# Layer 0's start reordered: input in four transfers, constants moved behind the normalisation, SyncE's transfers in source order

## The chip, the core and the metric

The kernel runs on one core of a Trainium2 chip. The metric is the device time of one execution in microseconds, taken as the median over runs. Five engines work side by side, each on its own list of instructions: TensorE (PE, with its weight loads PEld), VectorE (DVE), ScalarE (ACT), GpSimd (POOL) and SyncE (SP). SP computes nothing here; it issues transfers, and so does ACT in a few places.

## The reference

Two transformer layers work on 2048 tokens of 256 numbers, all in float32. Each layer is an attention block and a feed-forward block, both with a layer normalisation in front and a residual addition behind.

```python
x = x + attn0(layernorm(x), w_project, w_out)            # causal, 16 heads of 16
x = x + ffn0(layernorm(x), router_w, router_b, expert_w, expert_b)   # 8 experts, top 2 per output
x = x + attn1(layernorm(x), w_qkv, w_proj)               # 16 query heads, 4 key/value heads of 128
x = x + ffn1(layernorm(x), gate, up, down)               # 4-bit weights, gelu(gate) * up
return x

def layernorm(x, eps=1e-5):
    return (x - mean(x)) / sqrt(var(x) + eps)

def attn0(x, w_project, w_out):
    q, k, v = split(x @ w_project.T)
    att = softmax(where(causal, q @ k.T / sqrt(16), -1e9))
    return (att @ v) @ w_out.T
```

Only the start of layer 0's attention is touched by the change.

## The kernel before, in words

The residual `xres` stays in SBUF for the whole run as 16 tiles of 128 tokens by 256. Four tiles make a block, and layer 0 has four blocks, numbered `j` = 0 to 3. For each block the kernel normalises (`norm_pieces`: statistics L180 and L181 on VectorE, the power -1/2 L185 on GpSimd, the scaling L194 to `xn` on VectorE), transposes on TensorE (`inputs_T`, L210), and projects to queries and keys (`project`, L545) and values (`values`, L567). `project` copies its product from PSUM into a tile `stage` (L549), and eight transfers (L555) then spread `stage` over the tile `qk`, 16 partitions each. For block 0 half of these transfers are issued by ScalarE, for the others all by SyncE.

The attention runs in 40 batches `n`. Each is `greatest` (scores, L647), `mask` (the causal mask on TensorE, L660, and the row maxima on VectorE, L666), `shift` (L676, L679), `powers` (scores again, L695, and the exponentials, L704) and `mixed` (L731); `divided` (L749 to L788) closes a head group. Between these, `fill` hands out pieces of other work (the next block's normalisation and projections, layer 0's feed-forward) by fixed budgets per slot, so the order of instructions on TensorE, VectorE, ScalarE and GpSimd is the order of the source: `manual_schedule(engines=order)` pins them. SyncE is not in that set. The scheduler may place its transfers anywhere that their data allow.

The work before the first batch, in source order: identity and small constants (`mask32` L86, `fold8` L91, `mask8` L95, of which the last two serve layer 1 only), VectorE's presets of `va` (L481) and `bs` (L497), GpSimd's presets of `qk`, three products on TensorE that nobody reads (`idle`, L795, on the weights `wp`), the normalisation of blocks 0 and 1 in a row, GpSimd's presets for block 1 and its splitting of the biases (L518 to L529), block 0's projections, then block 1's transposes, and the first batch's scores. Block 2's normalisation is handed out in the first `fill` of batch 1.

SyncE's loads are written at the end of the batches:

```python
if n < 4:
    w, dram = (rw, router_w) if n < 2 else (ew, expert_w)
    for i in range(4):
        load_pair(w, dram, 4 * n % 8 + i)
...
if n in (0, 2):
    load_x(n // 2 + 2)
```

`load_pair` pins each transfer behind the SyncE instruction that was traced just before it. So the four pairs of batches 0 and 2 stand behind the `qk` transfers of block 1, while `load_x(2)` and `load_x(3)`, which need nothing, and the pairs of batches 1 and 3, which are pinned only behind these, are placed early by the scheduler.

Of the kernel before, what the change touches and what calls it, by code (L numbers as in the profile page):

```python
# [32 lines left out]
def tile_transformer(  # L33
# [26 lines left out]
    def load_x(j):  # L60
        nc.sync.dma_start(
            out=xres[:, 4 * j : 4 * j + 4, :], in_=x[:, 4 * j : 4 * j + 4, :]
        )

    for t, eng in ((0, nc.sync), (2, nc.scalar)):
        eng.dma_start(out=xres[:, t : t + 2, :], in_=x[:, t : t + 2, :])
    in_order = ctx.enter_context(ExitStack())
    order = {
        mybir.EngineType.PE, mybir.EngineType.DVE, mybir.EngineType.Pool,
        mybir.EngineType.Activation,  # L70
    }
    in_order.enter_context(tc.manual_schedule(engines=order))
    ident = const.tile([P, P], F32, name="ident")
    make_identity(nc, ident)
    minus_half = const.tile([P, 4], F32, name="minus_half")
# [12 lines left out]
    )  # L88

    fold8 = const.tile([P, 8], F32, name="fold8")  # L90
    nc.vector.tensor_reduce(  # L91
        fold8, ident.rearrange("p (t b) -> p b t", b=8), AX.X, ALU.add
    )
    mask8 = const.tile([P, NS, 8], F32, name="mask8")
    nc.vector.tensor_copy(mask8, fold8.unsqueeze(1).to_broadcast([P, NS, 8]))  # L95

# [350 lines left out]
    with ExitStack() as l0:  # L449
# [28 lines left out]
                    mask32[:, i : i + 1].to_broadcast([P, 512]),  # L478
                )

        nc.vector.memset(va[:, :per_block], 1.0)  # L481
        nc.gpsimd.tensor_copy(
            qk[:, :, 0].rearrange("p g s q -> p g (s q)"),
            mask32[:, :4].unsqueeze(2).to_broadcast([P, 4, 512]),
# [9 lines left out]
            base=0, pattern=[[-1, P]], channel_multiplier=1,  # L494
        )
        bs = b1.tile([P, 2, 512], F32, tag="hi4", name="bs")
        nc.vector.memset(bs, 0.0)  # L497
        for i in range(3):
            nc.sync.dma_start(out=bs[32 * i : 32 * i + 8], in_=bias)
        rows = b1.tile([P, 12, P], BF16, tag="part", name="rows")  # L500
        sel = rows[:, :8]
        bp = rows[:, 8:].rearrange("p i q -> p (i q)")
# [1 line left out]
        def blanks(xn):  # L504

            after = b2.tile([P, 1], F32, tag="rs_v", name="after")
            nc.gpsimd.tensor_copy(after, xn[:, 3, 0:1])
            for i in range(2):
                nc.gpsimd.memset(maxes[i], 0.0)
            nc.gpsimd.memset(qk[:, :, NBLK + 1].rearrange("p g s q -> p g (s q)"), 0.0)  # L510
# [19 lines left out]

        def load_pair(w, dram, n):
            e, hc = divmod(n, 2)
            tc.keep_in_program_order(
                nc.sync.dma_start(
                    out=w[:, hc, 2 * e : 2 * e + 2],
                    in_=dram[hc * P : (hc + 1) * P, 2 * e : 2 * e + 2],
                )
            )

        def project(j, xT, half, stage, i):  # L540

            at = 256 * (1 - i) + 128 * half
            ps = ps_dn.tile([P, 512], F32, tag="dn", name=f"qk_ps{j}_{half}_{i}")
            for hc in range(2):
                nc.tensor.matmul(  # L545
                    ps, lhsT=wp[:, hc, at : at + P],
                    rhs=xT[:, hc].rearrange("p s q -> p (s q)"), start=hc == 0, stop=hc == 1,
                )
            nc.scalar.copy(stage[:, i], ps)  # L549
            if i:  # L550
                to = 4 + j % 2
                for r in range(8):
                    h = 32 * (r % 4)
                    eng = nc.scalar if j == 0 and r % 2 else nc.sync
                    eng.dma_start(  # L555
                        out=qk[h + 4 : h + 20, 2 * half + r // 4, j : to + 1 : to - j].rearrange(
                            "p i s q -> p i (s q)"
                        ),
                        in_=stage[16 * r : 16 * r + 16],
                    )  # L560

        def values(j, xT, s):

            ps = ps_dn.tile([P, 2, HID], F32, tag="dn", name=f"v_ps{j}_{s}")
            for i in range(2):
                for hc in range(2):
                    nc.tensor.matmul(  # L567
                        ps[:, i], lhsT=xT[:, hc, s + i], rhs=wp[:, hc, 512:768],
                        start=hc == 0, stop=hc == 1,
                    )  # L570
            at = j * per_block
            to = va[:, at : at + per_block].rearrange("p (s h d) -> p s h d", s=NS, d=17)
            nc.scalar.copy(
                to[:, s : s + 2, :, 0:16], ps.rearrange("p s (h d) -> p s h d", d=16)
            )

# [13 lines left out]
        def projections(j, xT):  # L590
            if j > 1:
                for s in (0, 2):
                    yield need("PE", 1.75, 1, cond=lambda: blanked > 5 * j - 10)
                    values(j, xT, s)
            for half in range(2):
                if j or half:
                    stage = a1.tile([P, 2, 512], F32, tag="stage", name=f"stage{j}_{half}")
                else:
                    stage = unused("stage0", "p (i q) -> p i q", i=2)
                for i in range(2):  # L600

                    yield need(
                        "PE", 1.75, 0 if half or i else 1,
                        cond=lambda: j < 2 or done >= 8 * j - 12 and blanked >= 5 * j - 5,
                    )
                    project(j, xT, half, stage, i)
                if half == (not j) and j < 2:
                    for s in (0, 2):
                        yield need("PE", 1.75)
                        values(j, xT, s)  # L610

        def prepare(j):

            out = []
            yield from norm_pieces(
                j, b1, b2, out, cond=lambda: j == 2 or inputs[2].next is None
            )
            xT = a1.tile([P, 2, NS, P], F32, tag="xT0", name=f"xT0_{j}")
            yield from inputs_T(j, out[0], xT)
            yield from projections(j, xT)  # L620

        def unused(name, pattern, **sizes):

# [167 lines left out]


        ps = ps_mm.tile([P, 4, P], F32, tag="mm", name="idle")
        for i in range(3):
            nc.tensor.matmul(  # L795
                ps.rearrange("p b q -> p (b q)"), lhsT=ident, rhs=wp[:, 0, :512],
                start=not i, stop=i == 2,
            )
        load_x(1)
        nc.sync.dma_start(out=wo, in_=w_out.rearrange("(k p) o -> p k o", p=P))  # L800
        both = [[], []]
        for j in range(2):
            for piece in norm_pieces(j, b1, b2, both[j]):
                pass
            normed.clear()
            if not j:
                blanks(both[0][0])
                xT = a1.tile([P, 2, NS, P], F32, tag="xT0", name="xT0_0")
                for piece in inputs_T(0, both[0][0], xT):
                    pass  # L810
        for i in range(5):
            blank(1, i)
        split_biases()
        for piece in projections(0, xT):
            pass
        xT = unused("xT0_1", "p (h s q) -> p h s q", h=2, s=NS)
        for piece in inputs_T(1, both[1][0], xT):
            pass
        greatest(0)
        mask(0)  # L820
# [7 lines left out]
        for n in range(NBT):  # L828
            j, s, gs = batches[n]
            if n in (1, 7):  # L830
                to = 2 if n == 1 else 3
                inputs[to] = Stream(prepare(to))
                streams.insert(0, inputs[to])
            if n + 1 < NBT and batches[n + 1][0] != j:
                while inputs[j + 1].next is not None:
                    fill(PE=2.0, DVE=2.0)
            with tc.high_priority(offset=AHEAD):
                if n + 1 < NBT:
                    greatest(n + 1)
                shift(n)  # L840
                if n + 1 < NBT:
                    mask(n + 1)

            fill(PE=(2.0, 2.0, 1.8, 1.6)[j], DVE=2.6)
            with tc.high_priority(offset=AHEAD):
                if n:
                    mixed(n - 1)
                powers(n)
            done += 1
            if n and batches[n - 1][2][-1] == 3:  # L850
                streams.insert(0, Stream(divided(*batches[n - 1][:2])))
            fill(PE=(2.4, 2.4, 2.2, 2.0)[j], DVE=2.6)
# [4 lines that stand above are left out]
                    loaded[n // 2, (4 * n % 8 + i) // 2] = slot  # L857
            for _ in range(1 + (n < 2) if blanked < 10 else 0):
                blank(2 + blanked // 5, (blanked + 4) % 5)
                blanked += 1  # L860
            if n in (0, 2):
                load_x(n // 2 + 2)
        mixed(NBT - 1)
        streams.insert(0, Stream(norm_pieces(0, b1, b2, normed_first)))
        last = Stream(divided(*batches[NBT - 1][:2]))
# [436 lines left out]
```

## Time and profile before

| what | value |
|---|---|
| median of 3 runs | 1177.23 us (1175.32 to 1181.05) |
| the profiled execution | 1182.05 us |
| its span, first to last instruction | 1180.3 us |
| mean granted TensorE clock | 0.993 |
| TensorE busy | 1148.1 us, 97% of the span |
| VectorE busy | 809.7 us, 69% |
| ScalarE busy | 484.3 us, 41% |
| GpSimd busy | 108.1 us, 9% |
| chain that ended last | PE 79%, DVE 15%, ACT 2%, issue 2%, POOL 1%, DMA 1% |

The profile is one execution, so its own time is what a sum of its durations is held against. A span that starts at 0 is the first instruction's start. Idle time of an engine counts only where the chain of waits passes through it.

### The profile page before, as it was taken

The page shows a single profiled execution, that of the slowest core. Times are in us where ns is not written, and L with a number is a line of the kernel's source. Part 1 is how long each engine was busy: PE and PEld are TensorE (multiplying, and loading weights), DVE is VectorE, ACT ScalarE, POOL GpSimd, SP SyncE. Part 2 cuts the span into 40 slices and gives each one's busy share as a digit, 9 for nine tenths or more (in the row PEclk, how much of TensorE's full clock was granted, in tenths as well). Part 3 has the DMA queues.
Part 4 walks back from the last instruction along what each step waited for, and adds up shares of the span by engine and source line. Part 5 has one row for each costly group of instructions (what it writes and reads, how often), then busy time and mean ns, then how long its engine had stood idle before and what let it go on. Part 6 is the DMA issues. An engine that isn't in the chain of part 4 may idle for free.

```text
span 1180.3 us, 18580 instructions
## 1 busy us (share of the span) xinstructions
PE 1148.1 (97%) x7178; PEld 663.9 (56%) x7178; DVE 809.7 (69%) x1783; ACT 484.3 (41%) x1099; POOL 108.1 (9%) x152
## 2 busy tenths in 40 slices
PE   7999989999999899999999999999999999999998
PEld 3656545555555445555555556565644465485487
DVE  5656869999989872867872685687599844725710
ACT  1434545555565453444444443555244312303300
POOL 7313212111111100000000000000000000000000
PEclk9989989999999999999999999999999999999999
DMA  7320010000000320000000001020020000000000
GB/s 217 68 67 12 10 28 1 1 1 2 2 1 2 113 66 1 1 1 1 1 1 1 1 1 45 19 58 24 21 50 3 0 1 18 0 1 18 1 13 23
DMA packets 21239, 26.46 MB, mean 22 GB/s; under 512 B 5128, under 2 KB 14600, under 8 KB 21152
## 3 DMA queue, kind: packets, MB, share of 16 engines
q1 hardware_dynamic: 20480, 24.10, 7.6%
q10 hardware_dynamic: 672, 1.18, 0.4%
q8 instruction: 56, 0.92, 0.3%
q14 instruction: 31, 0.25, 0.1%
HBM read 18.97 MB, written 2.10 MB: 18 GB/s over the span
## 4 chain that ended last, share of the span: by engine, by line
PE 79%; DVE 15%; ACT 2%; issue 2%; POOL 1%; DMA 1%; SPq 0%; ACTq 0%; DVEq 0%; POOLq 0%
PE qk_ps L982 11%; PE y L1229 9%; PE o L1073 9%; PE g L911 9%; PE u L911 9%; PE lg_ps L234 8%; PE eo L234 7%; DVE mx L666 3%; PE s L647 3%; PE s L695 3%; PE av L731 2%; PE qk_ps L545 2%; PE v_ps L964 2%; PE a L1053 1%; PE s L995 1%
## 5 line engine op out<-in xcount | busy, mean ns | idle before, releaser
L982 PE MATMUL qk_ps<-xT,wqkv 128*128 128x512 f32 x320 | 148.9, 599 | 2.3 <-ACT part L323 1.2
L234 PE MATMUL lg_ps<-rw,xT 128*128 128x512 f32 x256 | 122.5, 601 | 1.3 <-ACT xT L949 0.3
L234 PE MATMUL eo<-ew,xT 128*128 128x512 f32 x256 | 121.5, 600 | 0.8 <-ACT lg L297 0.5
L1073 PE MATMUL o<-wpj,oT 128*128 128x256 f32 x512 | 119.1, 382 | 0.0
L1229 PE MATMUL y<-wd,it 128*128 128x256 f32 x512 | 111.8, 379 | 0.0
L1073 PEld LDWEIGHTS o<-wpj,oT 128*128 128x128 f32 x512 | 95.9, 190 | 27.5 <-issue 14.3
L1229 PEld LDWEIGHTS y<-wd,it 128*128 128x128 f32 x512 | 97.0, 190 | 15.0 <-issue 2.2
L666 DVE TENSOR_REDUCE mx<-s 128x1 f32<-128x384 f32 (+3 forms) x176 | 100.4, 631 | 1.4 <-PE s L660 1.4
L982 PEld LDWEIGHTS qk_ps<-xT,wqkv 128*128 128x128 f32 x320 | 59.1, 190 | 71.4 <-issue 57.4
L704 ACT ACTIVATE pt<-s 128x512 f32<-128x512 f32 (+1 forms) x176 | 84.1, 564 | 36.3 <-PE s L695 36.3
L911 PE MATMUL g<-xT,wgu 128*128 128x512 f32 x192 | 90.4, 593 | 0.0
L911 PE MATMUL u<-xT,wgu 128*128 128x512 f32 x192 | 90.2, 592 | 0.0
L323 ACT ACTIVATE part<-eo,c 128x256 f32<-128x256 f32 x128 | 53.6, 472 | 84.7 <-PE eo L234 77.1
L714 POOL TENSOR_SCALAR_AFFINE_SELECT pt<-pt 128x256 f32<-128x256 f32 (+2 forms) x88 | 62.8, 720 | 261.9 <-ACT pt L704 261.3
L1207 ACT ACTIVATE th<-sq 128x512 f32<-128x512 f32 x64 | 40.3, 630 | 87.6 <-DVE sq L1206 87.6
L234 PEld LDWEIGHTS lg_ps<-rw,xT 128*128 128x128 f32 x256 | 46.1, 190 | 46.1 <-issue 37.3
L234 PEld LDWEIGHTS eo<-ew,xT 128*128 128x128 f32 x256 | 46.1, 190 | 45.7 <-issue 38.3
L222 DVE TENSOR_TENSOR xres<-xres,y 128x256 f32<-128x256 f32 x16 | 6.7, 421 | 92.5 <-PE y L1229 92.5
L185 POOL TENSOR_TENSOR ln_rs<-rs_v,minus_half 128x4 f32<-128x4 f32 x16 | 17.6, 1100 | 552.2 <-DVE rs_v L184 439.8
L297 ACT COPY lg<-lg_ps 128x512 f32<-128x512 f32 x64 | 37.6, 588 | 73.5 <-PE lg_ps L234 73.5
L1208 DVE SCALAR_TENSOR_TENSOR th<-th,g 128x512 f32<-128x512 f32 x63 | 43.1, 684 | 29.3 <-ACT th L1207 29.2
L911 PEld LDWEIGHTS u<-xT,wgu 128*128 128x128 f32 x192 | 36.5, 190 | 45.9 <-issue 44.7
(233 smaller groups left out, 1784.4 us busy)
## 6 DMA issues: line engine op xcount, KB each, us to landing
qk<-stage SPq DMA_DIRECT2D x56, 64.0 KB, 2.4
wqkv<-in_w_qkv SPq DMA_DIRECT2D x8, 320.0 KB, 6.6
rw<-in_router_w SPq DMA_DIRECT2D x8, 256.0 KB, 6.9
ew<-in_expert_w SPq DMA_DIRECT2D x8, 256.0 KB, 5.0
wpj<-in_w_proj SPq DMA_DIRECT2D x1, 2048.0 KB
out<-xres SPq DMA_DIRECT2D x4, 512.0 KB, 2.6
xres<-in_x SPq DMA_DIRECT2D x3, 512.0 KB, 8.5
dq_wgu<-in_gate_w SPq DMA_DIRECT2D x8, 128.0 KB, 2.4
```

The lines of the kernel that those rows point to most:

```text
L234: nc.tensor.matmul(ps, lhsT=xT[:, hc, (g % 4) * P : (g % 4 + 1) * P], rhs=w[:, hc, 2 * pair : 2 * pair + 2, :].rearrange("p e o -> p (e o) ...
L297: nc.scalar.copy(lg[:, 2 * pair : 2 * pair + 2, :].rearrange("p e o -> p (e o)"), ps)
L323: nc.scalar.mul(part[:, e % 4], ps[:, i], c[:, e : e + 1])
L666: nc.vector.tensor_reduce(maxes[n % 2][:, h, gs[0] : gs[0] + nb], ps[:, : nb * nk].rearrange("p (b k) -> p b k", b=nb), AX.X, ALU.max,)
L704: nc.scalar.activation(pt[:, i, : nb * nk], tiles[2 * pair + i][:, : nb * nk], AF.Exp, scale=0.25)
L714: nc.gpsimd.affine_select(out=last, in_=last, compare_op=ALU.is_ge, fill=0.0, base=0, pattern=pattern, channel_multiplier=-1,)
L911: nc.tensor.matmul(ps, lhsT=wgu[:, w, half, jj, par * P : (par + 1) * P], rhs=xT[:, half, :], start=half == 0, stop=half == 1,)
L982: nc.tensor.matmul(ps, lhsT=wqkv[:, hc, kv, h, :], rhs=xT[:, hc, :], start=hc == 0, stop=hc == 1,)
L1073: nc.tensor.matmul(ys[t // 2][:, t % 2], lhsT=state["o"][:, h, t * P : (t + 1) * P], rhs=wpj[:, HPK * kv + h, :], start=kv == 0 and h == 0 ...
L1207: nc.scalar.activation(th, sq, AF.Tanh, scale=0.7978845608028654)
L1208: nc.vector.scalar_tensor_tensor(th, th, 1.0, gp, ALU.add, ALU.mult)
L1229: nc.tensor.matmul(ps, lhsT=it[:, c // 2, c % 2, t * P : (t + 1) * P], rhs=wd[:, c // 2, c % 2, :], start=c == 0, stop=c == 2 * NJ - 1,)
```

## The change

Six edits. First, the four tiles of block 0 come in four transfers of one tile, two issued by SyncE and two by ScalarE, where there were two transfers of two tiles. Secondly, `fold8`, `mask8`, the preset of `bs` with its three transfers, and VectorE's preset of `va` move behind block 0's normalisation or further. Thirdly, block 0's normalisation is written out in two halves of two tiles, each with its own power on GpSimd. Fourthly, the products that nobody reads run on the identity instead of `wp`, five of them instead of three. Fifthly, block 1's normalisation is split around the first half of block 0's projections, and the copies of that block's second half and of its values go from ScalarE to VectorE. Sixthly, SyncE's transfers are pinned to the order of the source from the start to the end of batch 3, and `load_pair` no longer pins by itself.

```diff
-    for t, eng in ((0, nc.sync), (2, nc.scalar)):
-        eng.dma_start(out=xres[:, t : t + 2, :], in_=x[:, t : t + 2, :])
+    for t in range(4):
+        eng = nc.scalar if t % 2 else nc.sync
+        eng.dma_start(out=xres[:, t, :], in_=x[:, t, :])
...
+    loads_in_order = ctx.enter_context(ExitStack())
+    loads_in_order.enter_context(tc.manual_schedule(engines={mybir.EngineType.SP}))
...
     fold8 = const.tile([P, 8], F32, name="fold8")
-    nc.vector.tensor_reduce(
-        fold8, ident.rearrange("p (t b) -> p b t", b=8), AX.X, ALU.add
-    )
     mask8 = const.tile([P, NS, 8], F32, name="mask8")
-    nc.vector.tensor_copy(mask8, fold8.unsqueeze(1).to_broadcast([P, NS, 8]))
...
-        nc.vector.memset(va[:, :per_block], 1.0)
...
         bs = b1.tile([P, 2, 512], F32, tag="hi4", name="bs")
-        nc.vector.memset(bs, 0.0)
-        for i in range(3):
-            nc.sync.dma_start(out=bs[32 * i : 32 * i + 8], in_=bias)
...
-            tc.keep_in_program_order(
-                nc.sync.dma_start(
-                    out=w[:, hc, 2 * e : 2 * e + 2],
-                    in_=dram[hc * P : (hc + 1) * P, 2 * e : 2 * e + 2],
-                )
+            nc.sync.dma_start(
+                out=w[:, hc, 2 * e : 2 * e + 2],
+                in_=dram[hc * P : (hc + 1) * P, 2 * e : 2 * e + 2],
             )
...
-            nc.scalar.copy(stage[:, i], ps)
+            (nc.scalar.copy if j or not half else nc.vector.tensor_copy)(stage[:, i], ps)
...
-            nc.scalar.copy(
+            (nc.scalar.copy if j else nc.vector.tensor_copy)(
                 to[:, s : s + 2, :, 0:16], ps.rearrange("p s (h d) -> p s h d", d=16)
             )
...
+        def normed_by_twos():
+
+            xn = b1.tile([P, 4, HID], F32, tag="xn", name="xn0_0")
+            st = b2.tile([P, 4, 6], F32, tag="ln_st", name="ln_st0_0")
+            mv = b2.tile([P, 4, 2], F32, tag="ln_mv", name="ln_mv0_0")
+            roots = []
+            for two in (slice(0, 2), slice(2, 4)):
+                for t in range(two.start, two.stop):
+                    nc.vector.bn_stats(st[:, t, :], xres[:, t, :])
+                    nc.vector.bn_aggr(mv[:, t, :], st[:, t, :])
+                v = b2.tile([P, 4], F32, tag="rs_v", name=f"rs_v0_{two.start}")[:, :2]
+                rs = b2.tile([P, 4], F32, tag="ln_rs", name=f"ln_rs0_{two.start}")[:, :2]
+                nc.vector.tensor_scalar(v, mv[:, two, 1], EPS, None, ALU.add)
+                nc.gpsimd.tensor_tensor(rs, v, minus_half[:, :2], ALU.pow)
+                roots.append(rs)
+            for t in range(4):
+                nc.vector.tensor_scalar(
+                    xn[:, t, :], xres[:, t, :], mv[:, t, 0:1],
+                    roots[t // 2][:, t % 2 : t % 2 + 1], ALU.subtract, ALU.mult,
+                )
+            return xn
...
-        for i in range(3):
+        for i in range(5):
             nc.tensor.matmul(
-                ps.rearrange("p b q -> p (b q)"), lhsT=ident, rhs=wp[:, 0, :512],
-                start=not i, stop=i == 2,
+                ps, lhsT=ident, rhs=ident.unsqueeze(1).to_broadcast([P, 4, P]),
+                start=not i, stop=i == 4,
             )
         load_x(1)
         nc.sync.dma_start(out=wo, in_=w_out.rearrange("(k p) o -> p k o", p=P))
...
+        xn = normed_by_twos()
+        blanks(xn)
+        xT = a1.tile([P, 2, NS, P], F32, tag="xT0", name="xT0_0")
+        for piece in inputs_T(0, xn, xT):
+            pass
+        nc.vector.memset(bs, 0.0)
+        for i in range(3):
+            nc.sync.dma_start(out=bs[32 * i : 32 * i + 8], in_=bias)
+        nc.vector.memset(va[:, :per_block], 1.0)
+        second = []
+        norm_1 = norm_pieces(1, b1, b2, second)
+        for _ in range(3):
+            next(norm_1)
+        firsts_0 = projections(0, xT)
+        for _ in range(3):
+            next(firsts_0)
+        for piece in norm_1:
+            pass
+        normed.clear()
         for i in range(5):
             blank(1, i)
         split_biases()
-        for piece in projections(0, xT):
+        for piece in firsts_0:
             pass
+        nc.vector.tensor_reduce(
+            fold8, ident.rearrange("p (t b) -> p b t", b=8), AX.X, ALU.add
+        )
+        nc.vector.tensor_copy(mask8, fold8.unsqueeze(1).to_broadcast([P, NS, 8]))
         xT = unused("xT0_1", "p (h s q) -> p h s q", h=2, s=NS)
-        for piece in inputs_T(1, both[1][0], xT):
+        for piece in inputs_T(1, second[0], xT):
             pass
...
             if n in (0, 2):
                 load_x(n // 2 + 2)
+            if n == 3:
+                loads_in_order.close()
```

More of the change, by code (lines that the diff above doesn't have):

```diff
@@ L800, in tile_transformer @@
         nc.sync.dma_start(out=wo, in_=w_out.rearrange("(k p) o -> p k o", p=P))
[L801 to L810, printed above, removed]
+        xn = normed_by_twos()
[17 more added lines that the diff above has]
+        normed.clear()
         for i in range(5):
```

## The prediction

> **What bounds the kernel now.** I read the page's engine shares first, then the chain of waits of the first 80 us, then the timelines of SyncE, VectorE and TensorE around the places that the diff touches. The page:
>
> ```profile
> span 1180.3 us, 18580 instructions
> PE 1148.1 (97%) x7178; PEld 663.9 (56%) x7178; DVE 809.7 (69%) x1783; ACT 484.3 (41%) x1099; POOL 108.1 (9%) x152
> ...
> PE 79%; DVE 15%; ACT 2%; issue 2%; POOL 1%; DMA 1%; SPq 0%; ACTq 0%; DVEq 0%; POOLq 0%
> ```
>
> TensorE is busy for 97% of the span and works in a fixed order. So what the first 60 us win or lose moves all behind it by the same amount; nothing later has slack to swallow it. The chain (start, length, what; us):
>
> ```profile
> 2.16 3.41 DVE mask L95
> 5.57 0.46 DVE bs L497
> 6.04 0.30 DVE ln_st L180
> ...
> 9.46 1.38 DVE xn L194 x4
> ...
> 21.23 0.60 ACTq L555
> ...
> 27.33 0.49 PE s L647 x4
> ...
> 43.34 0.34 DVE ln_st L180
> ...
> 46.83 2.70 DVE xn L194 x3
> 49.63 0.71 DVE xn L194
> 50.39 0.34 PE x_ps L210
> ```
>
> Two stretches matter. Up to 28 us VectorE, then ScalarE's issuing of transfers, hold the first scores. From 43.34 to 50.39 the chain leaves TensorE for VectorE again: block 2's normalisation. Its input is long there, as SyncE's timeline tells:
>
> ```profile
> 2.67 0.63 SPq L61 DMA_DIRECT2D xres<-in_x  x1
> 3.34 3.94 SPq L534 DMA_DIRECT2D rw<-in_router_w  x4
> ...
> 36.51 5.08 SPq L555 DMA_DIRECT2D qk<-stage  x8
> 41.64 2.93 SPq L534 DMA_DIRECT2D rw<-in_router_w  x4
> ```
>
> Block 2 of `x` is issued at 2.67. The four pairs at 41.64 are those of batch 0, pinned behind the eight `qk` transfers of block 1.
>
> **The change part by part.**
>
> *Start to block 0's `xn`.* `mask8` (3.41 us on the chain), the preset of `va` and that of `bs` (0.46 on the chain) leave the front, and `fold8` (0.30). The statistics then wait for the input. Two transfers of 256 KB, issued at 0.81 and 0.80, landed 4.0 and 4.1 us later; the first two of 128 KB I put at 4.1, the others at 4.8. Four statistics at 0.53 each (6.04 to 8.1 before) end at about 6.6. But the two powers stand on GpSimd behind its presets, which end at 6.28 (L492 at 5.99, 0.29), and the one power in the trace took 1.02. Two columns instead of four: no row shows that; between half of it, 0.51, and 1.02; I take 1.02, since 128 x 4 numbers are too few to set its length. Powers at 6.3 to 8.4, the last two scalings (0.33 apart) end at 9.2. Before: 10.84. If the first scalings stall beside the second power it is 9.8. Gain 1.0 to 1.65, more if the power is shorter. The two more issues (0.43 each, one on SyncE, one on ScalarE) push `wp` from 6.7 and 6.9 to about 7.3; it is wanted at 10. The three transfers of `bs` go out behind its preset at 9.7 and are wanted by L519 at 18: nothing.
>
> *Idle products.* Before, they waited for `wp` until 7.07, took 4.85 and ended behind `xn`, so the transposes began at 11.76. On the identity they start at about 1.4; ten instructions at 0.85 cold and 0.43 warm end between 7.3 and 9.9, beside VectorE's work. Cost zero; if the clock came late, up to 0.7. Transposes 9.3, `xT` copies 9.5, first projection at 10.1 instead of 13.04: 2.9 us won.
>
> *Block 0's second half.* Before, ScalarE issued four transfers from 17.44 for 2.65 us, and only then copied (20.13); its next transfers started at 21.23. Now VectorE copies. Its queue: `xn` until 9.2, presets of `bs` and `va` 1.0 (two steps of 0.5), block 1's statistics 2.26 (10.76 to 13.02), power and its waits 1.3, four scalings beside GpSimd's copies 2.5 (14.31 for 2.53): 16.3. The products are there at 15.6 and 17.3 (13.04 to 18.5 before, moved by 2.9), so the copies (0.69, L582's row) end at 18.0 and the transfers go out 3.2 us earlier. Before, 6.06 us lay between their start and the last landing at 27.29, some of it SyncE's waiting for free semaphores; so the last of batch 0's scores moves by 3.2 to 3.6. The copies of `va` go to VectorE as well (0.69 each, 19.2 and 21.0) and no longer queue behind ScalarE's issuing: block 1's transposes go from 24.80 to about 20.7. Queued behind `va` on VectorE are then `fold8`, `mask8`, two `xT` copies and the row maxima, which want VectorE at 24.5.
>
> Here a rule can be weighed. `mask8` took 3.41 us where the row's 32 numbers need a tenth of that; GpSimd's L482 and L486 ran from 1.90 to 5.53 beside it. The Trainium skill (SBUF — State Buffer, Who interferes with whom) says that a VectorE copy in a two-port mode and a GpSimd instruction exclude each other for a whole instruction. At its new place GpSimd splits the biases, with pieces of at most 1.5 us. By the rule `mask8` waits for one piece, ends before 23.6 and costs nothing. By the row of 3.41 it ends at 25.5, the `xT` copies at 26.8, and 2 us of the gain are lost. I take the rule for size, as the gaps of 0.07 us between those pieces free the port, and keep 1 us of loss as the lower end.
>
> Sum of the start: 3.4 us earlier at the first maxima (28.18), range 2.3 to 3.9.
>
> *SyncE in source order.* This is a moved step, so its whole queue counts. In source order `load_x(2)` stands at the end of batch 0, behind block 1's eight `qk` transfers and four pairs of `rw`. That front part is already in the trace at its place: eight transfers 36.51 to 41.59 (0.64 each), four pairs until 44.57, the last of them landing at 48.27 (the trace's semaphore updates). Block 2's 512 KB queue behind; `wo` and block 2 landed 1.3 us apart at the start (8.81, 10.10), so block 2 lands at 49.6 on before's clock. VectorE asks for it at 43.25, right behind batch 1's maxima, in fixed order. Both times hang on block 1's `stage` copies, so the gap of 6.35 us does not depend on how much the start wins. Queued behind the waiting statistics on VectorE are L185's input, `rden`, `oq`, the scalings, `shift(2)` and batch 2's maxima; on GpSimd the power, and behind it the selections of `pt`; on TensorE L766, then L210. TensorE's slack there is 0.3 us (L210's wait). If the pairs moved at the rate of the early ones (0.78 us each) it would be 5.2; if block 2 also shared the engines with the pairs of batch 1 behind it, 7.4.
>
> *The clock.* TensorE would stand, but for 1.4 us of small work, from 49.3 to 57.9. What that does, the trace shows elsewhere:
>
> ```profile
> 76.98 0.38 PE L766 MATMUL oq_T<-ident,oq 128*128 128x128 f32 x2
> 80.21 3.78 PE L545 MATMUL qk_ps<-xT,wp 128*128 128x512 f32 x4 [2.85 <-ACT stage L549]
> 83.78 0.63 PE L252 MATMUL fold<-rows 128*128 128x512 bf16 x1
> 84.35 1.94 PE L731 MATMUL av<-pt,va 128*32 128x128 f32 x32
> ```
> ```profile
> 77.00:90.00 13.00, 10.15 (x91) 5.88 (x93) 4.49 (x9) 3.88 (x8) 0.97 (x2) 0.74 0.23 38
> ```
>
> A wait of 2.85 us, and the granted clock (0.74 over the stretch) was at half from 79.4 to 86.3; work of 3.15 us took 6.0, a loss of 2.85. The Trainium skill (TensorE: Matmul & The Clock Gate, What's actually happening) has the clock halve after an idle window of about 3.4 us and recover after one busy window. By the rule the wait of 2.85 should have cost nothing, and recovery 1.7 us; the row says that less idling is enough, and that it costs 2.85. For the new wait both say cold. Work resumes between two window ends, so 3.4 to 6.8 us of cold work, 1.7 to 3.4 lost, and 0.3 on the transposes: 2.8.
>
> *The rest.* The other pairs come in time: batch 1's `rw` land by about 55, wanted by L258 at 62.6 plus the shift; block 3 and the last `ew` by 72, wanted at 103 and 84. That leaves 2 us before the `qk` transfers of 71.21; if they collided, 1 us.
>
> Sum: -3.4 + 6.35 + 2.8 = +5.75 us. Against the profiled execution's own 1182.05 (span 1180.3 and 1.75 around it) that is 1187.8. The median of the runs, 1177.23, is 4.8 lower than that execution; the shift is applied to it: 1183.0.
>
> **The rivals.** *A: the loads come in time* (0.14). If SyncE's order left block 2 early after all, or its wait were covered, only the start's 3.4 us remain: 1173.8. For it: `load_x(2)` depends on nothing, and the scheduler has had it at 2.67. Against: pinning is what the edit says. *B: slower by more* (0.13). One mechanism: the start's gain fails at VectorE. If `mask8` stalls for 3.4 us at its new place (past 24.5 us it decides) and the scalings stall beside the power, the start wins 1, and the wait and clock remain: -1 + 6.9 + 3.1 = +9, 1186.2, with a second cold window +11. *C: faster* (0.03): block 2 in time, and the `qk` transfers, freed from the loads of `rw` and `ew` that ran until 18.4, land 3 us sooner: 1171. *The main case* (0.70): +5.75, own range +2.5 to +8.7, 1179.7 to 1185.9.
>
> **How the numbers follow.** A difference of 0.5%, 5.9 us, is about what a measurement of this kernel can tell from no change. The main case lies on that line, so its chance is cut in half: slower 0.36 and B 0.13, with rounding 0.50; same 0.34 and most of A, 0.45; faster 0.05. The range takes the main case whole, most of B, and the part of A above 1175.5: 1175.5 to 1189.5. The likeliest case's own range is 1179.7 to 1185.9.
>
> **What would show it.** Right: first statistics at about 4.2, first projection near 10, batch 0's maxima near 24.8, `load_x(2)` issued at about 41, L180 of block 2 waiting some 6 us for `xres<-in_x`, TensorE idle for 6 to 8 us around 46 to 54, and a stretch of halved clock behind. Wrong: no wait of VectorE on `xres` there, a `mask8` of over 2 us that the maxima wait for, or a start that wins under 2 us.

## The result and the profile after

The changed kernel takes 1185.64 us (median of 6 runs, 1184.27 to 1186.58), the kernel before 1177.14 us beside it (6 runs, 1175.32 to 1181.05). The ratio is 1.0070, with a 95% interval of 1.0053 to 1.0088: slower by 6.2 to 10.4 us. The profiled execution took 1185.63 us, with a span of 1183.9 us.

The page's shares alone would not give it away:

```profile
span 1183.9 us, 18593 instructions
PE 1151.7 (97%) x7182; PEld 665.2 (56%) x7182; DVE 812.4 (69%) x1788; ACT 482.2 (41%) x1095; POOL 108.9 (9%) x153
...
PE 79%; DVE 14%; issue 3%; POOL 2%; ACT 2%; DMA 1%; SPq 0%; ACTq 0%; DVEq 0%; POOLq 0%
```

In the chain "issue" grew from 2% to 3% and GpSimd from 1% to 2%, and VectorE fell from 15% to 14%. The chain's first 80 us, read in order of time, show both sides of the change (start, length, what):

```profile
6.27 1.51 POOL ln_rs L629 x2
7.80 0.75 DVE xn L632 x2
...
16.68 0.61 DVE stage L543
...
24.84 0.71 DVE mx L682 x2
...
38.42 11.46 issue
49.93 1.04 POOL ln_rs L185
...
52.09 2.42 DVE xn L194 x3
54.55 1.33 PE x_ps L210 x5
55.88 3.60 PE qk_ps L539 x4
```

The first row maxima (L682) start at 24.84. VectorE's timeline of the kernel before has them at 28.18:

```profile
28.18 2.48 DVE L666 TENSOR_REDUCE mx<-s 128x4 f32<-128x512 f32 x4 [1.40 <-PE s L660]
```

So the start won 3.34 us. Then come 11.46 us that the chain can only call "issue". What they are, VectorE's timeline tells at that place, and the table of waits up to 80 us repeats it:

```profile
47.41 0.43 DVE L180 BATCH_NORM_STATS2 ln_st<-xres 128x6 f32<-128x256 f32 x1 [7.41 <-DMA xres<-in_x]
```
```profile
DVE ln_st L180 <- DMA xres<-in_x: 7.4, 1, 7.4
```

VectorE reached block 2's statistics at 40.0 and stood until 47.41, since block 2 was not there. SyncE's timeline shows why:

```profile
33.18 5.55 SPq L549 DMA_DIRECT2D qk<-stage  x8
38.77 2.01 SPq L529 DMA_DIRECT2D rw<-in_router_w  x4
40.83 0.43 SPq L61 DMA_DIRECT2D xres<-in_x  x1
41.30 2.67 SPq L529 DMA_DIRECT2D rw<-in_router_w  x4
```

In source order `load_x(2)` goes out at 40.83, where it went out at 2.67 before, and it landed at 47.39 by the trace's semaphore updates. TensorE's timeline shows what follows:

```profile
50.60 0.66 PE L782 MATMUL oq_T<-ident,oq 128*128 128x128 f32 x2 [4.48 <-DVE oq L773]
52.32 0.45 PE L210 MATMUL x_ps<-ident,xn 128*128 128x128 f32 x1 [1.05 <-DVE xn L194]
53.32 2.56 PE L210 MATMUL x_ps<-ident,xn 128*128 128x128 f32 x7 [0.56 <-DVE xn L194]
55.70 3.78 PE L539 MATMUL qk_ps<-xT,wp 128*128 128x512 f32 x4
```

TensorE stands for 4.48, 1.05 and 0.56 us, and the next projection takes 3.78 us. In the kernel before, the same four products took 1.98 at full clock:

```profile
51.39 1.98 PE L545 MATMUL qk_ps<-xT,wp 128*128 128x512 f32 x4 [0.24 <-ACT xT L582]
```

The window view puts the granted clock of the stretch beside it (length, busy time of PE, PEld, DVE, ACT, POOL with counts, clock, share and rate of the DMA engines):

```profile
50.40:60.50 10.10, 8.01 (x31) 3.70 (x34) 7.10 (x11) 2.13 (x4) 3.95 (x5) 0.50 0.01 2
```

The clock was at half for about 10 us. The values of block 2 start at 62.78 (L561) where they started at 56.13 (L567), by TensorE's timelines of before and after:

```profile
56.13 1.89 PE L567 MATMUL v_ps<-wp,xT 128*128 128x256 f32 x8
```
```profile
62.78 1.89 PE L561 MATMUL v_ps<-wp,xT 128*128 128x256 f32 x8
```

The start's -3.34 and the wait's +7.41 make about +4.1, and the clock adds 2.5, together +6.65. Before the mask of batch 5 the shift is still +6.65 (76.54 to 83.19). By the end of the span it is only +3.6, because the profiled execution of before had two stretches of half clock behind that, of 6.8 us each (from 79.45 and from 151.13), and that of after had two of half that length (from 87.89 and from 156.16).

### The profile page after: what moved, and what is told of

The parts are those of the page before. It is cut to its first block, busy times and chain, and to the rows that moved or that the text cites. A ratio compares the mean times of both kernels' runs of the same rounds, so it can differ in the third digit from the quotient of the medians.

```text
span 1183.9 us, 18593 instructions
## 1 busy us (share of the span) xinstructions
PE 1151.7 (97%) x7182; PEld 665.2 (56%) x7182; DVE 812.4 (69%) x1788; ACT 482.2 (41%) x1095; POOL 108.9 (9%) x153
## 4 chain that ended last, share of the span: by engine, by line
PE 79%; DVE 14%; issue 3%; POOL 2%; ACT 2%; DMA 1%; SPq 0%; ACTq 0%; DVEq 0%; POOLq 0%
PE qk_ps L1013 11%; PE y L1260 9%; PE o L1104 9%; PE g L942 9%; PE u L942 9%; PE lg_ps L234 8%; PE eo L234 7%; DVE mx L682 3%; PE s L711 3%; PE s L663 3%; PE av L747 2%; PE qk_ps L539 2%; PE v_ps L995 2%; PE a L1084 1%; PE s L1026 1%
## 5 line engine op out<-in xcount | busy, mean ns | idle before, releaser
L682 DVE TENSOR_REDUCE mx<-s 128x1 f32<-128x384 f32 (+3 forms) x176 | 100.4, 632 | 0.1
```

The source lines that it names most:

```text
L682: nc.vector.tensor_reduce(maxes[n % 2][:, h, gs[0] : gs[0] + nb], ps[:, : nb * nk].rearrange("p (b k) -> p b k", b=nb), AX.X, ALU.max,)
```

## The experiments

Each kernel was run beside the kernel before. The median of before differs a little from one experiment to another (1178.55 to 1179.4), so ratios are compared.

**e1: block 2 issued at the start, all else as in after.**

```diff
         nc.sync.dma_start(out=wo, in_=w_out.rearrange("(k p) o -> p k o", p=P))
+        load_x(2)
...
-            if n in (0, 2):
-                load_x(n // 2 + 2)
+            if n == 2:
+                load_x(3)
```

> The changed kernel with one line moved: block 2 of x is loaded right behind w_out at the start instead of at the end of batch 0. Theory (the late block 2 is the whole loss): VectorE's wait of 7.5 us on xres at batch 1 and the halved clock behind it vanish, the start's 3.3 us stay, so about 1173.8 us, 3.3 below before and some 12 below the changed kernel. Rival 1 (part of the loss lies behind 85 us, since the two profiles differ by less than the medians): about 1175.6. Rival 2 (the loads of rw and ew, now late, cost by themselves through the folds or the qk transfers): 1180 or more.

Measured: 1173.25 us (6 runs, 1172.69 to 1174.19), ratio to before 0.9949 (0.9934 to 0.9964). VectorE's timeline has the first maxima at 25.13, and block 2's statistics start at 40.21 without a wait:

```profile
25.13 2.48 DVE L682 TENSOR_REDUCE mx<-s 128x4 f32<-128x512 f32 x4 [0.42 <-PE s L676]
...
40.21 0.42 DVE L180 BATCH_NORM_STATS2 ln_st<-xres 128x6 f32<-128x256 f32 x1
```

TensorE's timeline has only this left at the place:

```profile
47.34 0.77 PE L210 MATMUL x_ps<-ident,xn 128*128 128x128 f32 x5 [0.29 <-DVE xn L194]
```

The mean granted clock was 1.000 in this execution. The window view of the same stretch, first after, then e1:

```profile
43.00:58.00 15.00, 8.63 (x53) 4.43 (x52) 9.32 (x20) 2.80 (x6) 4.42 (x5) 0.74 0.39 124
```
```profile
43.00:58.00 15.00, 14.47 (x160) 9.66 (x159) 11.43 (x19) 7.19 (x14) 6.84 (x8) 1.00 0.57 149
```

TensorE works 14.47 of 15 us instead of 8.63. One transfer, moved, turns a loss of 0.7% into a gain of 0.5%. The place of `load_x(2)` is the cause of the loss. The gain is larger than expected: 6 us against the runs of before beside it, where the theory had 3.3 and the first maxima moved by 3.05. The mean granted clock of e1's six runs is 0.997 to 1.000 (median 0.9995) against a median of 0.996 in before's runs; at the 0.85 us for each 0.001 that before's runs show further down (with e9), I estimate that this makes the other 3 us.

**e2: the order alone, on the kernel before** (edits one to five left out).

```diff
+    loads_in_order = ctx.enter_context(ExitStack())
+    loads_in_order.enter_context(tc.manual_schedule(engines={mybir.EngineType.SP}))
...
-            tc.keep_in_program_order(
-                nc.sync.dma_start(
+            nc.sync.dma_start(
...
+            if n == 3:
+                loads_in_order.close()
```

> The kernel before with SyncE's source order as the only edit (pinned from the start to the end of batch 3, load_pair without its own pin). Theory: the wait of 7.5 us and 2.5 us of cold clock are its own doing and do not depend on the other edits, so about 1187 us, +10; the transfers of bs now stand ahead of block 1's load and wait for VectorE's preset, which may add up to 1. Rival (the wait hurts only because the start became earlier): 1180 or less. Rival (taking rw and ew out of the first 18 us speeds up the first qk transfers): 1 to 3 us less than 1187.

Measured: 1187.67 us (1186.93 to 1190.73), ratio 1.0076 (1.0059 to 1.0092). VectorE and TensorE show the same pair of waits on their timelines:

```profile
51.18 0.43 DVE L183 BATCH_NORM_STATS2 ln_st<-xres 128x6 f32<-128x256 f32 x1 [7.56 <-DMA xres<-in_x]
```
```profile
54.37 0.66 PE L767 MATMUL oq_T<-ident,oq 128*128 128x128 f32 x2 [4.64 <-DVE oq L758]
```

The first maxima are at 28.46, so the order by itself wins nothing at the start, and the clock was again at half for 10 us (52.7 to 63.0). The order alone gives the whole loss.

**e3: edits one to five without the order** (guard and closing removed, `load_pair` pinned as before).

```diff
-    loads_in_order = ctx.enter_context(ExitStack())
-    loads_in_order.enter_context(tc.manual_schedule(engines={mybir.EngineType.SP}))
...
+            tc.keep_in_program_order(
...
-            if n == 3:
-                loads_in_order.close()
```

> The changed kernel without SyncE's source order (pins as before, so the scheduler places block 2 and half of the pairs early). Theory: the other five edits win 3.3 us and nothing is late, 1173.8. Rival (the loads of rw and ew, early again, slow the qk transfers that now come 3 us sooner and collide with them): half of the gain is lost, 1175.5. Rival (part of the loss is in the start's edits themselves): no faster than 1177.

Measured: 1181.61 us (22 runs, 1175.33 to 1183.5), ratio 1.0011 (0.9999 to 1.0022). The theory missed by some 8 us, and the rival was right, with more force than it claimed. VectorE's timeline:

```profile
27.34 2.48 DVE L681 TENSOR_REDUCE mx<-s 128x4 f32<-128x512 f32 x4 [3.49 <-PE s L675]
```

The first maxima win 0.84 us, not 3.34. Two views show what holds them, SyncE's timeline and its waits (total, times, longest):

```profile
4.16 3.50 SPq L527 DMA_DIRECT2D rw<-in_router_w  x4
7.70 0.43 SPq L61 DMA_DIRECT2D xres<-in_x  x1
8.45 3.02 SPq L527 DMA_DIRECT2D ew<-in_expert_w  x4
12.23 1.83 SPq L823 DMA_DIRECT2D bs<-in_bias  x3
```
```profile
SPq L548 <- DMA ew<-in_expert_w: 2.6, 2, 1.7
```

Without the order the scheduler again puts four `rw` loads, block 3 and four `ew` loads at the start. A `qk` transfer needs none of them, and yet SyncE waits for `ew`. By the trace's records the kernel's transfers, SyncE's and ScalarE's together, take turns on eight completion semaphores, and each late issue below carries the semaphore of the load that it stands behind: a new transfer goes out when the earlier one with its semaphore has landed. ScalarE's timeline has the same, in e3 and then in after:

```profile
15.15 8.15 ACTq L548 DMA_DIRECT2D qk<-stage  x8
```
```profile
14.00 6.75 ACTq L549 DMA_DIRECT2D qk<-stage  x8
```

In both the copy of `stage` starts at 13.34. In e3 the first issue comes at 15.15, just behind block 3's landing at 15.05. Of the next five on the two queues, four stand as closely behind landings of `ew` (15.82 behind 15.75, 16.43 behind 16.41, 17.47 behind 17.46, 18.86 behind 18.84). The last of block 0's sixteen issues goes out at 22.71, in after at 20.15: 2.56 us, which is what the maxima lose. The transfers themselves take about as long in both (2.9 to 3.9 us from issue to landing in after, 2.4 to 4.2 in e3).

**e11: the same loads put early on purpose, on e1.**

```diff
         load_x(2)
+        for i in range(4, 8):
+            load_pair(rw, router_w, i)
+        load_x(3)
+        for i in range(4, 8):
+            load_pair(ew, expert_w, i)
...
-                    load_pair(w, dram, 4 * n % 8 + i)
+                    if n % 2 == 0:
+                        load_pair(w, dram, 4 * n % 8 + i)
...
-            if n == 2:
-                load_x(3)
```

> The kernel with block 2 loaded at the start, with batch 1's four pairs of rw, block 3 and batch 3's four pairs of ew also put at the start, right behind block 2, in pinned order. Theory (the first qk transfers must wait for a completion semaphore held by a load that is still under way; without the order the trace shows issues at 15.15, 16.43, 17.47 and 18.86 just behind landings at 15.05, 16.41, 17.46 and 18.84): the first maxima move from 25.1 back to about 27.3, and TensorE's wait for them can drop the clock as in the kernel without the order: 1175.5 to 1181. Rival (the kernel without the order lost its gain otherwise, by where the scheduler put the transfers of bs): 1173 to 1174.

Measured: 1181.1 us (14 runs, 1175.34 to 1183.72), ratio 1.0017 (1.0004 to 1.0029), where e1 has 0.9949.

```profile
27.52 1.89 DVE L682 TENSOR_REDUCE mx<-s 128x4 f32<-128x512 f32 x3 [4.02 <-PE s L676]
```

The maxima are back at 27.52 (25.13 in e1), and the first `qk` issues stand at 14.78, 15.48, 16.11, 16.78 and 18.23, all five within 0.1 us behind landings of the loads (14.68, 15.40, 16.09, 16.77, 18.21). Here the cause is put in by hand, with SyncE in order and block 2 in time, and gives e3's time. So the early loads are what e3 loses by. What in them costs the time is not separated: they hold the semaphores, and they also keep the DMA engines busy (a share of 1.0 from 7 to 17 us in e3 and e11, 0.3 in after), so that an earlier issue might have had to queue. It also says that the order of SyncE is not simply bad: it keeps these loads out of the way of the `qk` transfers, which is worth 2.4 to 2.5 us at the maxima.

**e5: block 2 ahead of batch 0's pairs, a half dose** (block 3 as in e1).

```diff
+            if n == 0:
+                load_x(2)
...
-            if n in (0, 2):
-                load_x(n // 2 + 2)
+            if n == 2:
+                load_x(3)
```

> The changed kernel with block 2's load moved ahead of batch 0's four pairs, not to the start: one dose of the same wait. Theory: issued at 38.8 instead of 40.8 and with nothing ahead in the rings but the qk transfers, it lands near 42.6 and is wanted at 39.9, so 2.7 us of the wait stay; TensorE idles about 2 us less than 3, so the clock may or may not fall (0 to 1.5): 1176.5 to 1178. Rival (the order as such costs, not this wait): 1184 or more.

Measured: 1181.47 us (22 runs, 1178.71 to 1183.61), ratio 1.0019 (1.0010 to 1.0027). The wait came out at the size expected:

```profile
43.96 0.43 DVE L180 BATCH_NORM_STATS2 ln_st<-xres 128x6 f32<-128x256 f32 x1 [2.37 <-DMA xres<-in_x]
```

The time did not: it misses by some 4 us. In the profiled execution the clock was at half at 27.0 to 30.4, 50.9 to 54.3, 81.6 to 88.5 and 153.3 to 156.7, the last two at waits that before and after have too. Only the second has to do with block 2. Block 2's values start at 58.00 in this execution and at 53.08 in e1's, 4.92 later: VectorE asks 1.38 later, behind the first fall, it waits 2.37, and the second fall makes the other 1.2. So the wait costs its own length, and what a run costs beyond it hangs on how often the clock falls.

**e6: TensorE kept at work during the first part of the wait** (five more products on the identity behind the mask of batch 3, on after).

```diff
+                if n == 2:
+                    warm = ps_sc.tile([P, 512], F32, tag="sc", name="warm")
+                    for i in range(5):
+                        nc.tensor.matmul(
+                            warm.rearrange("p (b q) -> p b q", b=4), lhsT=ident,
+                            rhs=ident.unsqueeze(1).to_broadcast([P, 4, P]),
+                            start=not i, stop=i == 4,
+                        )
```

> The changed kernel with five products on the identity put in front of the transposes that stall in batch 2, in a score tile that nobody reads; they fill 4.3 us of TensorE's 4.48 us idle time while VectorE waits for block 2, and change nothing else. Theory (wait and clock are two prices): the wait of 7.4 us stays, the granted clock doesn't fall at 50, the 2.5 us behind it come back: 1185.6 before it on the first chip, 2.5 below the changed kernel's +8.5, so +6 against before. Rival (the clock was not what made the products after the wait slow, or the filler delays the transposes): no change, +8.5.

Measured: 1185.74 us (6 runs, 1182.79 to 1187.99), ratio 1.0072 (1.0057 to 1.0087): no gain that can be measured. TensorE's timeline and windows of the profiled run:

```profile
46.02 4.46 PE L875 MATMUL warm<-ident 128*128 128x512 f32 x10
50.45 0.41 PE L782 MATMUL oq_T<-ident,oq 128*128 128x128 f32 x2
52.16 0.30 PE L210 MATMUL x_ps<-ident,xn 128*128 128x128 f32 x1 [1.30 <-DVE xn L194]
53.16 0.33 PE L210 MATMUL x_ps<-ident,xn 128*128 128x128 f32 x1 [0.70 <-DVE xn L194]
```
```profile
54.60:58.00 3.40, 3.40 (x8) 1.76 (x7) 2.73 (x5) 1.17 (x2) 0.00 (x0) 0.50 0.00 0
```

The products fill the 4.5 us before L782, but behind it, where TensorE has only short waits on `xn` and small products, the clock fell all the same, for 3.4 us instead of 10. Block 2's values start at 61.42 in this execution, 1.4 us earlier than in after. So the clock's part is smaller in this one execution, the median does not show it, and how much a fully covered wait would give back was not tried.

**e7 and e8: a spare tile for the first half of block 2's `stage`,** on e1 and on the kernel before. Block 2's first half then goes to a tile that nothing uses at the time, and TensorE need not wait for `stage` at the place where both versions stand.

```diff
-                if j or half:
+                if j % 2 or half or j > 2:
...
-                    stage = unused("stage0", "p (i q) -> p i q", i=2)
+                    stage = unused(f"stage{j}", "p (i q) -> p i q", i=2)
```

> The kernel with block 2 loaded at the start, and block 2's first half of queries and keys staged in an unused tile instead of the single stage buffer. Theory: TensorE's wait of 2.35 us near 77 (the second half's copy waits for the first half's eight transfers) goes, and nothing else depends on it: 1173.25 - 2.3 = 1171. Rival (the chain then waits for something next to it, such as the transfers' own pace on SyncE): 1172.5 or more.

> The kernel before with the same spare staging tile as its only edit. Theory (the clock falls at short waits in some executions only, and this spreads before's runs from 1175.7 to 1182.6): without the wait of 2.85 us near 77 the clock can't fall there, so 2.85 us go in each run and up to 2.85 more in those where it fell: 3 to 5.7 us below before's median, with less spread. Rival (the spread is from elsewhere): 2.85 us less and the same spread of 7 us.

Measured: e7 1171.38 us (6 runs, 1170.96 to 1174.17), ratio 0.9950 (0.9937 to 0.9964), the lowest median of all, though its ratio is not apart from e1's. In e1 TensorE waited here, and in e7 the second half of the projection follows without a wait:

```profile
76.67 1.98 PE L539 MATMUL qk_ps<-xT,wp 128*128 128x512 f32 x4 [2.35 <-ACT stage L543]
```
```profile
73.61 0.38 PE L782 MATMUL oq_T<-ident,oq 128*128 128x128 f32 x2
73.83 1.88 PE L539 MATMUL qk_ps<-xT,wp 128*128 128x512 f32 x4
```

e8 took 1175.26 us (22 runs), ratio 0.9967 (0.9959 to 0.9976). Its runs stand in two groups: nine from 1172.56 to 1172.86, thirteen from 1175.06 to 1176.47, where before's 27 runs beside it spread over 7.8 us (1175.31 to 1183.15) without such a gap in the middle. Every run also has its mean granted clock: 0.998 to 1.000 in the lower group, 0.996 to 0.998 in the upper one. The profiled run is one of the upper group. TensorE's timeline has one wait of that kind left, and the window behind it is at half clock:

```profile
146.13 2.93 PE L545 MATMUL qk_ps<-xT,wp 128*128 128x512 f32 x3 [2.97 <-ACT stage L549]
```
```profile
145.40:152.10 6.70, 5.97 (x43) 2.99 (x47) 1.50 (x8) 4.10 (x16) 0.00 (x0) 0.50 0.04 6
```

**e9: e3 once more.**

> The changed kernel without the source order once more, for a second profile: its 22 runs lay from 1175.3 to 1183.5 and the profiled one was the fastest. Theory (the clock's falls at 27, 79 and 148 us make the spread): a run near 1181 shows one or two more stretches at half clock than the first profile's single one, each 3.4 or 6.8 us long, with TensorE's waits of the same length as there. Rival: the waits themselves are longer.

Measured: 1176.89 us, one run. The clock was at half twice (24.5 to 31.3, 198.6 to 202.0). The upper group of e3's times (around 1182) was not caught with a profile, so where its falls lie is not shown. That it is falls, the runs do tell: over e3's 22 runs the time follows the mean granted clock, from 1175.3 at 0.999 to between 1182.7 and 1183.5 at 0.990 to 0.991. A straight line through the runs of a kernel, worked out by least squares, gives:

| kernel | runs | time at full clock | us for 0.001 of mean clock | correlation |
|---|---|---|---|---|
| before, beside all experiments | 89 | 1175.9 | 0.85 | -0.88 |
| e3, no order | 22 | 1174.4 | 0.94 | -0.95 |
| e11, loads early | 14 | 1174.2 | 0.95 | -0.92 |
| e8, before with a spare tile | 22 | 1172.6 | 0.94 | -0.94 |
| e5, block 2 ahead of the pairs | 22 | 1176.8 | 0.75 | -0.86 |

By these lines e3 is 1.5 us faster than before at full clock; the maxima that come 0.84 earlier are part of it. Its measured median is slower because its median clock is 0.993, that of before 0.996.

**e10: block 0's copies back on ScalarE, on e1.**

```diff
-            (nc.scalar.copy if j or not half else nc.vector.tensor_copy)(stage[:, i], ps)
+            nc.scalar.copy(stage[:, i], ps)
...
-            (nc.scalar.copy if j else nc.vector.tensor_copy)(
+            nc.scalar.copy(
```

> The kernel with block 2 loaded at the start, and the copies of block 0's second half and of its values back on ScalarE, behind its four transfer issues. Theory (those issues hold the copies): the copies start when the issues end at about 17 instead of 16.6, the second half's transfers go out about 0.4 later than 17.9, block 1's transposes wait for values copied behind four more issues (until about 22), so the first maxima come 0.3 to 1 us later than 25.1, and the time is 0.3 to 1 above 1173.25. Rival (this edit is what won most of the start): 2 to 3 us more.

Measured: 1174.6 us (5 runs, 1174.45 to 1175.88), ratio 0.9964 (0.9951 to 0.9976); the interval overlaps e1's.

```profile
24.83 2.48 DVE L682 TENSOR_REDUCE mx<-s 128x4 f32<-128x512 f32 x4 [1.48 <-PE s L676]
```

The maxima start at 24.83 with the copies on ScalarE, 24.84 in after and 25.13 in e1 with them on VectorE. ScalarE's queue has its four issues done before the second half's copies at 16.74, and the transfers leave at 17.88, in after at 17.91. So this part of the fifth edit is worth nothing at the first maxima, and the 0.3 to 1 us that the theory gave it there did not show. Behind them e10's execution runs up to 1.3 us later than e1's (block 2's statistics at 41.52 against 40.21), with a fall of the clock from 26.9 to 30.3 between; whether the copies have a part in that is open. The gain comes from the earlier first projection and from the late loads.

## Why the prediction was right, and where it was not

*The start, -3.4 at the first maxima.* It was -3.34. Inside the sum errors cancelled. The first statistics began at 3.57, not 4.1 to 4.2. The powers of two columns took 0.71 and 0.83 us; I had taken the upper bound of 1.02, on the ground that so few numbers don't set the length, and they do. The first projection began at 9.60, not 10.1. Against that, VectorE's presets of `bs` and `va` (0.91 and 0.96, with gaps of 0.16 and 0.17) were done at about 10.7, and not 10.2; GpSimd's preset of `qk` ran from 9.08 to 10.88 beside them. The second half's transfers left at 17.91, for 18.0.

*The owner of that gain.* This step failed. I gave the whole 3.4 us to edits one to five, and counted the absence of early `rw` and `ew` loads only in rival C, as something that would come on top. e3 has the five edits and 0.84 us. e2 has the order and nothing. Both together have 3.34: the five edits make the `qk` transfers ready earlier, and the order keeps the loads of `rw` and `ew`, their semaphores and their load on the DMA engines, out of the way. The number was right and its reason half right.

*`mask8` at its new place, by the rule or by the row of 3.41.* The rule was the better guide. GpSimd's and VectorE's rows of after at the place:

```profile
21.76 0.60 POOL L518 COPY rows<-bh 32x512 bf16<-32x512 bf16 x1
22.34 1.15 POOL L519 TENSOR_TENSOR br<-bs,bh 96x512 f32<-96x512 f32 x1
```
```profile
22.11 1.42 DVE L844 COPY mask<-fold 128x32 f32<-128x32 f32 x1
23.45 1.28 DVE L576 COPY xT<-x_ps 128x512 f32<-128x512 f32 x2
```

It took 1.42 us, not 3.41, and cost the maxima nothing. But it began at 22.11 beside L518, which ran until 22.36, and ended at 23.53, just behind L519 (23.49): it sat through the rest of one GpSimd piece and the whole of the next. In the kernel before it did the same, from 2.16 to 5.57 beside L482 (until 3.79) and L486 (until 5.53). The Trainium skill (SBUF — State Buffer, Who interferes with whom) has the one that comes second wait for a whole instruction of the other; both rows agree with a full block, and both show it lasting into a second instruction. My reason, that the gaps between the pieces free the port, is thus not borne out: no gap shows between L518 and L519, and in both rows the length is that of what was left of one piece and of the whole next one. Rival B, which needed 3.4 us here, did not happen, although the time came close to its 1186.2.

*Block 2's lateness, 6.35 us.* The mechanism and the place were right, the term was 1.05 too small: 7.41. Block 2 did land 1.26 us behind the last pair, for the 1.3 that I took. But the last of the four pairs landed 7.36 us behind the first one's issue instead of 6.63, and SyncE came to the pairs 5.59 us behind its first `qk` issue of block 1 instead of 5.13; the two make 1.2, of which smaller differences take 0.1 back. Batch 1's four pairs were issued right behind block 2, from 41.30, and block 2 took 6.6 us from issue to landing. The size is that of the case with shared engines that I had priced at 7.4 as an end of the range; that the sharing made it is not shown.

*The clock, an estimate of 2.8 us.* It was 2.5, over a stretch of 10.2 us at half clock, longer than the 6.8 that I allowed; TensorE had only 8.0 us of work in it, so the loss is less than half of it. The Trainium skill (TensorE: Matmul & The Clock Gate, What's actually happening) speaks of one busy window for recovery; here it took three intervals of 3.4 us.

*The sum.* +5.75 became +6.65 behind block 2 by the trace. The median moved by 8.5 (6.2 to 10.4). The step that I treated as harmless is the shift from the profiled execution to the median: I added the change to a median of three runs of before. In the 89 later runs before's median is 1178.78, and 1178.78 + 6.65 is 1185.4, against 1185.64 measured. So part of the 8.5 is probably a low first reading of before. The further loads (`rw` of batch 1, the `ew` pairs, block 3) came in time, as said.

## What to carry to other kernels

- When transfers are pinned to source order, look for the load that depends on nothing and is written late: here one 512 KB load had been hoisted by 38 us, and putting it at the start by hand turned the change from 0.7% slower to 0.5% faster.
- Loads that are hoisted too eagerly cost as well (2.4 to 2.5 us at the first maxima here): they hold completion semaphores that urgent transfers must take in turn, and they fill the DMA engines. Put each load ahead of its need, and behind the first critical transfers.
- Read a kernel that is bound by TensorE by its granted clock, run by run. A wait of 2 to 3 us on TensorE can cost up to twice its length (2.85 us and as much again behind it in the kernel before), and removing that one (e8) won 2.8 to 4.8 us by the interval of its ratio.

## What the runs showed of the hardware

- Waits of nearly the same length dropped the clock in some executions and not in others: 2.93 and 2.99 us in e9 and 2.35 in e1 without a fall, 2.97 in e8, 2.60 in after and 2.51 in e10 with one. The traces' clock records tell more than their lengths do. The clock changes only at the marks of a grid of 3.41 us that runs through the whole execution: in after the falls and returns stand at 50.34, 60.58, 87.89, 91.30, 156.16 and 159.57, that is 0, 3, 11, 12, 31 and 32 steps of 3.413 us behind the first. The other traces fit such a grid as well, and where it stands against the first instruction differs from run to run. So a wait that fills most of one step drops the clock (e8's began at 143.2, in the step that ended at 145.3), and one of the same length that lies across two steps may not (e9's 2.93 lies across the mark at 79.09).
- How much work a step must hold can be estimated from the traces. Count each product at its length at full clock (0.43 us for 512 columns of float32, half of it for bfloat16) times the share of the array's 128 rows that it uses, so that a score product on 32 rows counts a quarter. The twelve traces have 4008 steps between 20 and 1160 us. All 36 with half clock in the step behind them hold less than 0.375 of what a step at full clock can hold; of the other 3972, all but three (0.365 each) hold more. The same measure tells how long a fall lasts: e3's at 26.7 was over after one step that held 0.383, e11's at 25.7 went on through steps of 0.327 and 0.364, though in both TensorE's row shows it busy throughout, with many products on 32 rows. This count was fitted to the traces afterwards; no run was made to test it.
- A kernel's spread over runs is then mostly the number of its falls: 0.75 to 0.95 us for each 0.001 of mean clock in the five kernels with 14 runs or more. A change to TensorE's waits can shift the distribution or split it in two groups (e8), which one profiled execution cannot show.
- A transfer's issue can wait for the landing of an unrelated one, since SyncE's and ScalarE's transfers share eight completion semaphores in turn (15.15 behind 15.05, 15.82 behind 15.75, 16.43 behind 16.41, 17.47 behind 17.46, 18.86 behind 18.84 in e3). On the timeline that appears as a queue that starts late, with no reason in its own data.
